# A routed two-layer network on one core: product 4 of the first layer by seven of its own blocks, and another order of the last products

## The chip, the cores and the metric

The kernel runs on one core of a Trainium2 chip. The core has a matrix engine (TensorE, PE in the profile), a vector engine (VectorE, DVE), a scalar engine (ScalarE, ACT), a general engine (GpSimd, POOL) and a sync engine (SyncE, SP) that here only issues DMAs. TensorE writes its results to PSUM, which has eight banks of 512 fp32 values in each of 128 partitions; VectorE and ScalarE read them there, GpSimd does not. Each engine runs its own queue in order and waits on semaphores that the others raise. The metric is device time in microseconds of one execution. Three runs of the kernel before gave 1569.73, 1569.85 and 1571.15 us; the median is 1569.85 us.

## The reference

The input is 4096 rows of 512 values. Each row is rotated by a quaternion product with two constant sides (in exact arithmetic one 4 x 4 mix of the row's four parts), a gate picks two of eight experts for it and two weights, and each expert takes its first 1024 rows. In an expert a row goes through two layers, and its result comes back weighted and is added to the input:

```python
logits = xf @ gate_w.T
topv, topi = jax.lax.top_k(jax.nn.softmax(logits, axis=-1), 2)
...
h = jax.nn.relu(jnp.einsum('ecd,ehd->ech', de, fc1_w) + fc1_b)   # 8 x 1024 x 2048, over 512
eo = jnp.einsum('ech,ehd->ecd', h, fc2_w) + fc2_b                # 8 x 1024 x 512, over 2048
out = x + jnp.sum(eo.reshape(E * cap, Dm)[flat_idx] * (gates * w)[:, :, None], axis=1)
```

All of it is fp32.

## The kernel before

**Order of the whole.** The routing comes first: logits, choice, ranks, and three lists of row numbers for 8 x 1024 slots. Then two generators are run in turns, `first_layers()` and `second_layers()`, which write out the engines' queues by hand (`tc.manual_schedule()`). The work is cut into 32 groups, k = 0 to 31: expert e = k // 4 and quarter g = k % 4 of its 2048 hidden units. A group's first layer (`layer1`, for group 0 `layer1_plain`) is 14 units, i = 0 to 13, one `yield` each. A group's second layer is two halves (`st0` = 0 and 2) of 7 units each. One turn is one unit of the first layer and then one unit of the second layer of the group before; in PE's queue they alternate. At turn i of group k the second layer's unit is: 0 `start` of st0 = 0 of group k-1 (with 1 and 2 still the last two of group k-2), 3 to 6 its products 1, 5, 4, 6, 7 `start` of st0 = 2, 8 product 3, 9 product 2, and 10 to 13 products 1, 5, 4, 6 of st0 = 2.

**Products of blocks.** Both layers multiply two matrices cut 2 x 2 by seven products of sums of blocks in place of eight (numbers 0 to 6; `left1`, `right2`, `sums` make the sums). A product of the first layer is 2 hidden tiles x 2 inner tiles of 128 x 128 weights against 512 slots. In the kernel before, products 0, 5 and 4 are done whole by `half` (L852): four matmuls of 512 columns. Products 1 and 6, and 3 and 2, are themselves done by seven blocks of 128 x 128 x 256 (`within`, L831, called in pairs by `pair`, L874); their sums of blocks come from `left_sub` (GpSimd, L146) and `right_sub` (VectorE, L162). The profile counts two passes for each fp32 matmul. A unit of the second layer (`product2`, L792) is four matmuls of 256 columns, eight passes.

**What VectorE does.** The first layer's results stand in SBUF in `beside` (h11, h21, r12) and `h22`. Each block's bank is added to one or two of them as soon as it is there (`add`, L886; L901, L907, L925, L917), and the next block with other signs accumulates onto the same bank: TensorE may write it again only when VectorE has read it. `chain` (L807) then makes three more sums for the second layer. The second layer's banks are added to `acc` (L1132 to L1216). The bank pools are `ps_1` (4 banks, first layer), `ps_2` (3, second layer) and `ps_x` (1, the next expert's input).

**What lies beside it.** `background` and `fetches` are lists of small steps of which `turn` (L785) runs so many after each unit as `PACE` (L1230) says for g and i, first number after the first layer's unit, second after the second layer's. In them are `chain`'s sums, the next expert's input (its rows gathered by GpSimd's indirect DMA, exchanged by 32 x 32 squares with SyncE's DMAs in `exchange`, turned by VectorE at L723 and mixed at L767, with ScalarE for the first term), and the stores of the expert before: `store` (L666) scales by the gate on ScalarE, adds to the gathered output rows on GpSimd (L669), and scatters them with an indirect DMA (L657). `TURN_OF_SUM` (L1022) says at which turns GpSimd makes the next group's four left sums.

**The end.** The last group's second layer runs alone (14 units), and the last half (`last`, L1167) is written apart: products 1, 5, 4, 6, 3, 2, where VectorE weighs each piece straight into the gathered rows (`weigh`, L650), and four scatters close the kernel. The first four tiles of the last expert still go through `store`.

Of the kernel before, what the change touches and what calls it, by code (L numbers as in the profile page):

```python
# [39 lines left out]
P = 128  # L40
D = 512
NJ = 4
E = 8
# [23 lines left out]
def kernel(  # L67
# [510 lines left out]
    vp = ctx.enter_context(tc.tile_pool(name="vp", bufs=3))  # L578
# [35 lines left out]
    beside = [hp.tile([P, 3, 2, HALF], F32, name=f"beside{i}") for i in range(2)]  # L614
    unused = [hp.tile([P, 2, HALF], F32, name=f"hidden{i}") for i in range(5)]
# [6 lines left out]
    class Rows:  # L622
# [43 lines left out]
        def store(self, st, acc):  # L666
            nc.scalar.activation(acc, acc, AF.Copy, scale=self.w[:, st : st + 1])
            r = self.rows[st]
            nc.gpsimd.tensor_tensor(r, acc, r, ALU.add)  # L669
            self.scatter(st)  # L670

    class Slots:
# [37 lines left out]
        def arrivals(self, half):  # L710

            n = PER if half == 0 else 2
            t = self.a if half == 0 else self.b
            for at in range(0, PER, n):
                for st in range(n):
                    yield lambda st=st, at=at: self.gather_ahead(t[:, st], half, at + st)
                yield from [lambda: None] * 2
                for b in range(QT):
                    yield lambda b=b, at=at: self.exchange(t, half, at, b)
                yield from [lambda: None] * 2  # L720
# [71 lines left out]
    def product2(out, st0, factors, n, first, tiles=range(2)):  # L792
# [11 lines left out]
        if st0 + 2 == PER and 1 in tiles and n in (2, 3, 4, 5):  # L804
            unused.append(factors[0][n])

    def chain(k, h22):  # L807


        h11, h21, r12 = (beside[k % 2][:, i] for i in range(3))  # L810
# [3 lines left out]
        def last():  # L814
# [7 lines left out]
            *[lambda: None] * (2 if k == NK - 1 else 0),  # L822
            last,
        ]

# [16 lines left out]
    def layer1(k, factors, subs):  # L842
# [5 lines left out]
        h11, h21, r12 = (h[:, i] for i in range(3))  # L848
# [25 lines left out]
        def pair(n, o, at, base, base_read):  # L874

            two = h[:, at : at + 2]
            t, u = bank1(f"t{n}_{k}"), bank1(f"u{n}_{k}")
            halves = t.rearrange("p (n s) -> p n s", n=2)  # L880

            def both(bank, i, first=False):
                within(bank[:, A], subs, n, i, first)
                within(bank[:, B], subs, o, i)

            def add(m, half):  # L886
                to = two[:, :, m, half]
                V.tensor_tensor(to, halves, to, ALU.add)  # L888

            within(base[:, A], subs, o, 1)  # L890
            within(base[:, B], subs, o, 2)
            base_read()
            both(t, 0, True)
            add(0, A)
            yield
            both(t, 5)
            add(0, B)
            both(u, 4, True)
            to = two[:, :, :, B]
            term = u.rearrange("p (n s) -> p n s", n=2).unsqueeze(2).to_broadcast([P, 2, 2, HS])  # L900
            V.tensor_tensor(to, term, to, ALU.add)  # L901
            yield
            both(t, 6)
            add(1, B)
            within(u[:, A], subs, n, 1, True)
            within(u[:, B], subs, n, 2)
            V.tensor_tensor(two[:, 0, 0], u, two[:, 0, 0], ALU.add)  # L907
            yield
            both(t, 3)
            add(1, A)  # L910
            relu(two[:, 0])

        def from5(m):
            nc.scalar.activation(h21[:, m], a[m], AF.Identity, bias=hi[:, m : m + 1])

        def from4(m):
            V.tensor_tensor(r12[:, m], b[m], r12[:, m], ALU.add)  # L917

        yield from pair(1, 6, 0, a[0], lambda: from5(0))
        yield  # L920
        h22 = unused.pop(0)
        b = [bank1(f"b{m}_{k}") for m in range(2)]
        for m in range(2):
            half(b[m], m, 4, True)
            V.tensor_tensor(h22[:, m], b[m], h21[:, m], ALU.add)  # L925
            if m == 1:
                from4(1)
                relu(h22)
            yield
        yield from pair(3, 2, 1, b[0], lambda: from4(0))  # L930
        chain(k, h22)
# [4 lines left out]
    def layer1_plain(k, w, x):  # L936
# [4 lines left out]
        h11, h21, r12 = (beside[k % 2][:, i] for i in range(3))  # L941
        h22 = unused.pop(0)
        for half in range(2):
# [6 lines left out]
            for at, i in ((at, i) for at in parts for i in range(NJ)):  # L950
# [22 lines left out]
                if half == 1 and done:  # L973
                    chain(k, h22)
# [3 lines left out]
    def first_layers():  # L978
# [43 lines left out]
        TURN_OF_SUM = {8: 2, 9: 0, 10: 1, 13: 3}  # L1022
        nxt = None
        for k in range(NK):
# [27 lines left out]
            if k:  # L1052
                for n, block, turns in (
                    (2, left_f[2], (2, 2, 3, 3)),
                    (3, w1_of[k][:, 1, 1], (4, 4, 5, 5)),
                ):
                    lefts[n], more = left_sub(k, n, block)
                    later(more, turns)
                if k == 1 or g == 0:
                    for n, turns in ((6, (1, 2, 2, 3)), (2, (4, 4, 5, 5)), (3, (6, 7, 8, 9))):  # L1060
                        right_subs[n], more = right_sub(xtp, e, n, xf[n])
                        later(more, turns)
# [6 lines left out]
            for i, _ in enumerate(units):  # L1069
# [3 lines left out]
                if k:  # L1073

                    if i == 8 and k + 1 < NK:
                        lefts[6], more = left_sub(k + 1, 6, left_n[6])
                        later(more, (9, 10, 11, 12))
                        lefts[1], more = left_sub(k + 1, 1, w1_of[k + 1][:, 0, 1])
                        later(more, (10, 11, 12, 13))
                        if g == NG - 1:  # L1080
                            right_subs[1], more = right_sub(xtp, e + 1, 1, xf_n[1])
                            later(more, (8, 9, 9, 12))
# [10 lines left out]
                if e + 1 < E:  # L1093

                    if (g, i) in ((0, 12 if e else 5), (1, 8)):
                        fetches.extend(nxt.arrivals(g))
                    if (g, i) in ((1, 11), (2, 9)):
# [22 lines left out]
    def second_layers():  # L1120
# [4 lines left out]

        def start(k, st0):
            e, g = divmod(k, NG)
            before = biases[e] if g == 0 else accs[st0]
            a = ps_2.tile([P, 2, DB], F32, tag="p2", name=f"a2_{k}_{st0}")
            v1 = vp.tile([P, 2, DB], F32, tag="v", name=f"v1_{k}_{st0}")  # L1130
            product2(a, st0, (hidden[k], rights[k]), 0, True)
            V.tensor_tensor(v1, a, before[:, :2, :DB], ALU.add)  # L1132
# [5 lines left out]
        for n, (k, st0) in enumerate(units):  # L1138
# [7 lines left out]
            if g == 2 and st0 == 0:  # L1146
                r = rows[e] = Rows(e)
                fetches.extend(lambda st=st, r=r: r.gather_choice(st) for st in range(SLOTS))
            if g == NG - 1 and st0 == 0:
                background.append(rows[e].weights)  # L1150
                fetches.extend(lambda st=st, r=rows[e]: r.gather_rows(st) for st in STORED)
# [10 lines left out]
            v2 = vp.tile([P, 2, DB], F32, tag="v", name=f"v2_{k}_{st0}")  # L1162
            product2(a, st0, factors, 5, False)
            V.tensor_tensor(v2, a, i12, ALU.add)
# [3 lines left out]
            if last:  # L1168
# [4 lines left out]
                for m in range(2):  # L1173
                    r.weigh(tiles[m], o11[:, m], LEFT)
                    r.weigh(tiles[m], v2[:, m], RIGHT)
                    r.weigh(tiles[2 + m], i21[:, m], LEFT)

                b = [
                    ps_2.tile([P, HALF], F32, tag="p2", name="b_top")[:, :DB],
                    ps_x.tile([P, HALF], F32, tag="xps", name="b_low")[:, :DB],  # L1180
                ]
            product2(b, st0, factors, 4, True)
            yield
            v3 = vp.tile([P, 2, DB], F32, tag="v", name=f"v3_{k}_{st0}")
            product2(a, st0, factors, 6, False)
            V.tensor_tensor(v3, a, i22, ALU.add)  # L1186
            for m in range(2) if last else [slice(0, 2)]:
                V.tensor_tensor(o22[:, m], b[m] if last else b, v3[:, m], ALU.add)
# [4 lines left out]
            if n + 1 < len(units):  # L1193
                ahead = start(*units[n + 1])
                yield
# [102 lines left out]
```

## Time and profile before

| | |
|---|---|
| median of three runs | 1569.85 us |
| the profiled execution: its time | 1569.29 us |
| the profiled execution: its span in the profile | 1567.4 us |
| granted TensorE clock, mean | 0.987 |
| PE busy | 1529.9 us, 98% of the span |
| DVE busy | 1152.7 us, 74% |
| POOL busy | 1048.7 us, 67% |
| ACT busy | 318.9 us, 20% |
| one group of steady state, k = 1 to 31 | 46.46 us |

The profile's page gives busy time by engine, then the span in 40 slices, then the groups of instructions by source line (L796 is line 796 of the kernel before). A line such as `PE b L796 <- DVE acc L1209: 0.6, 1, 0.6` in the list of waits says who waited for whom, how long in all, how often, and the longest. In the timeline a row is start, duration, engine, line, operation, output and inputs, count, and in brackets the idle time before it and who ended it. A matmul's duration in the timeline overlaps that of the next; what a stream of them costs is read from start to start.

### The profile page before, as it was taken

The numbers are of one execution on the slowest core, as the hardware profiler recorded it, in microseconds if no ns is written. First come the engines' busy times: TensorE is split into PE (matmuls) and PEld (weight loads), VectorE is DVE, ScalarE is ACT, GpSimd is POOL, SyncE is SP. The second block draws the span as 40 slices with busy tenths as digits, with TensorE's granted clock in tenths as the row PEclk, the third lists the DMA queues.
The fourth block names the chain that finished last, engine by engine and source line by source line (L and its number), as shares of the span: only waits on it lengthen the run. The fifth ranks groups of instructions, "written<-read, shape, count | busy, mean of one in ns | idle before, by whom it ended". The sixth has DMA issues, their size and how long they took to land.

```text
span 1567.4 us, 17504 instructions
## 1 busy us (share of the span) xinstructions
PE 1529.9 (98%) x6399; PEld 1190.9 (76%) x6399; DVE 1152.7 (74%) x1601; ACT 318.9 (20%) x450; POOL 1048.7 (67%) x1133
## 2 busy tenths in 40 slices
PE   5899999999999999999999999999999999999996
PEld 3677877877777787777887777787787787777785
DVE  6568886588856887578875888758886688866665
ACT  3222112221122112222112221122113121221110
POOL 1754687746977477965779468775697747794535
PEclk7899999999999999999999999999999999999998
DMA  8463123511334103531135311342133420331003
GB/s 324 160 212 94 55 68 117 140 59 55 113 97 139 62 28 114 148 116 55 33 104 159 93 55 61 121 123 79 55 102 102 139 64 28 114 107 54 11 17 106
DMA packets 79373, 152.18 MB, mean 97 GB/s; under 512 B 12022, under 2 KB 40950, under 8 KB 74168
## 3 DMA queue, kind: packets, MB, share of 16 engines
q1 hardware_dynamic: 56848, 90.24, 18.7%
q0 software_dynamic: 18048, 52.31, 10.8%
q10 hardware_dynamic: 4392, 8.52, 1.4%
q8 instruction: 50, 0.82, 0.2%
q14 instruction: 35, 0.29, 0.1%
HBM read 119.77 MB, written 25.23 MB: 93 GB/s over the span
## 4 chain that ended last, share of the span: by engine, by line
PE 91%; DVE 4%; issue 2%; DMA 2%; POOL 1%; SPq 0%; POOLq 0%; DVEq 0%
PE a L796 26%; PE b L796 20%; PE t L833 14%; PE a L854 12%; PE u L833 7%; PE b L854 7%; PE p L955 2%; PE b L833 2%; PE a L833 1%; DMA xb<-in_xt_dram 1%; DVE hidden L820 1%; DVE xa L767 1%; POOL rows L601 0%; DVE hidden L816 0%; POOL out_dram L657 0%
## 5 line engine op out<-in xcount | busy, mean ns | idle before, releaser
L796 PE MATMUL a<-t,hidden 128*128 128x256 f32 x1024 | 244.0, 382 | 5.3 <-DVE v L1186 5.2
L796 PEld LDWEIGHTS a<-t,hidden 128*128 128x128 f32 x1024 | 195.9, 191 | 58.5 <-issue 27.5
L888 DVE TENSOR_TENSOR beside<-t,beside 128x512 f32<-128x512 f32 x248 | 170.3, 687 | 94.3 <-PE t L833 90.4
L829 ACT ACTIVATE beside<-beside 128x1024 f32<-128x1024 f32 x62 | 65.5, 1057 | 558.0 <-DVE beside L888 558.0
L833 PE MATMUL t<-xsub,sub 128*128 128x256 f32 x496 | 127.9, 380 | 0.4
L796 PEld LDWEIGHTS b<-w,hidden 128*128 128x128 f32 x504 | 96.0, 190 | 38.9 <-issue 29.1
L796 PE MATMUL b<-w,beside 128*128 128x256 f32 x512 | 121.1, 380 | 0.6 <-DVE acc L1209 0.6
L796 PE MATMUL a<-t,beside 128*128 128x256 f32 x512 | 121.0, 379 | 0.0
L796 PE MATMUL a<-w,beside 128*128 128x256 f32 x512 | 121.0, 379 | 0.0
L796 PE MATMUL b<-t,hidden 128*128 128x256 f32 x504 | 119.1, 379 | 0.0
L796 PE MATMUL b<-w,hidden 128*128 128x256 f32 x504 | 119.1, 379 | 0.0
L796 PEld LDWEIGHTS b<-w,beside 128*128 128x128 f32 x512 | 97.4, 190 | 27.1 <-issue 15.7
L796 PEld LDWEIGHTS a<-w,beside 128*128 128x128 f32 x512 | 97.5, 190 | 26.2 <-issue 14.8
L854 PE MATMUL b<-x,s 128*128 128x512 f32 x248 | 116.6, 593 | 0.0
L854 PE MATMUL a<-x,s 128*128 128x512 f32 x248 | 116.6, 593 | 0.0
L854 PE MATMUL a<-xa,w 128*128 128x512 f32 x248 | 116.4, 593 | 0.0
L137 POOL TENSOR_TENSOR s<-w 128x512 f32<-128x512 f32 x31 | 39.5, 1274 | 112.7 <-PE b L854 112.7
L139 POOL TENSOR_TENSOR s<-w 128x512 f32<-128x512 f32 x31 | 39.8, 1283 | 111.3 <-PE t L833 111.3
L140 POOL TENSOR_TENSOR s<-w,s 128x512 f32<-128x512 f32 x31 | 39.4, 1270 | 107.5 <-PE t L833 101.9
L796 PEld LDWEIGHTS a<-t,beside 128*128 128x128 f32 x512 | 97.4, 190 | 13.1
L796 PEld LDWEIGHTS b<-t,hidden 128*128 128x128 f32 x504 | 96.0, 190 | 12.8
L833 PEld LDWEIGHTS t<-xsub,sub 128*128 128x128 f32 x496 | 94.0, 190 | 14.6 <-DVE beside L888 2.3
(233 smaller groups left out, 3089.4 us busy)
## 6 DMA issues: line engine op xcount, KB each, us to landing
w<-in_w_dram SPq DMA_DIRECT2D x64, 1024.0 KB, 5.1
xb<-in_xt_dram SPq DMA_DIRECT2D x8, 1024.0 KB, 9.9
out_dram<-in_x_dram ACTq DMA_DIRECT2D x1, 8192.0 KB
rows<-xa SPq DMA_DIRECT2D x112, 64.0 KB, 2.1
rows<-xb SPq DMA_DIRECT2D x224, 32.0 KB, 1.9
b<-in_b_dram POOLq DMA_DIRECT2D x8, 256.0 KB, 3.8
c<-choice,slot_cho POOLq DMA_INDIRECT x64, 2.3
rows<-out_dram,slot_tok POOLq DMA_INDIRECT x64, 3.5
```

The source lines that it names most:

```text
L137: lambda: G.tensor_tensor(s[0], w[:, 1, 0], w[:, 1, 1], ALU.add),
L139: lambda: G.tensor_tensor(s[2], w[:, 0, 0], w[:, 1, 0], ALU.subtract),
L140: lambda: G.tensor_tensor(s[3], w[:, 0, 1], s[1], ALU.subtract),
L767: V.scalar_tensor_tensor(to, t, M[:, i, j : j + 1], to, ALU.mult, ALU.add)
L796: nc.tensor.matmul(out[m] if isinstance(out, list) else out[:, m], lhsT=factors[0][n][:, c, (st0 + m) * P : (st0 + m + 1) * P], rhs=factor ...
L820: lambda: V.tensor_tensor(s2, s1, h11, ALU.subtract),
L829: nc.scalar.activation(h, h, AF.Relu)
L833: nc.tensor.matmul(out, lhsT=subs[0][n][i], rhs=subs[1][n][i], start=first, stop=True, skip_group_check=True,)
L854: nc.tensor.matmul(out, lhsT=factors[0][n][:, c, m * P : (m + 1) * P], rhs=factors[1][n][:, c, :], start=first and c == 0, stop=c == 1, sk ...
L888: V.tensor_tensor(to, halves, to, ALU.add)
L955: nc.tensor.matmul(ps[n][m][:, at], lhsT=w[:, block, i // 2, i % 2, m * P : (m + 1) * P], rhs=x.of(half, i)[:, at], start=i == 0 and at.st ...
```

## The change

Product 4 of the first layer is no longer done whole. It is done by its own seven blocks, in turns 8 to 11 (the four pieces of the diff that end in `yield`): blocks 1 and 2 go into a bank `b` (which then also takes product 2's blocks 1 and 2), blocks 0, 5, 6 and 3 go one after the other into the left half of a bank `t4`, and block 4 into the right half of the same bank. VectorE adds each from there to h22 and r12 together (`add_to_both`), and h22 now lies in `beside`. `left_sub` and `right_sub` make the sums for product 4 too. The turns of the other sums, of the gathers and exchanges for the next expert (`ARRIVE`: at turn i of g, gather or exchange of a part), of its turning and mixing, and `PACE` are set anew; `o12` and `o22` are summed in `acc` itself instead of in `v2` and `v3`.

For the last expert the output rows are gathered one group sooner, `store` is one VectorE operation (`weigh`) and a scatter, and the last half's products go in the order 1, 5, 4, 6, 2, 3 with each 256-column piece in a bank of its own.

```diff
-    beside = [hp.tile([P, 3, 2, HALF], F32, name=f"beside{i}") for i in range(2)]
-    unused = [hp.tile([P, 2, HALF], F32, name=f"hidden{i}") for i in range(5)]
+    beside = [hp.tile([P, 4, 2, HALF], F32, name=f"beside{i}") for i in range(2)]
+    unused = [hp.tile([P, 2, HALF], F32, name=f"hidden{i}") for i in range(3)]
...
         def store(self, st, acc):
+            if self.e == E - 1:
+                self.weigh(st, acc)
+                self.scatter(st)
+                return
...
+            if n == 2 and waiting:
+                background.insert(0, waiting.pop())
...
-            *[lambda: None] * (2 if k == NK - 1 else 0),
-            last,
         ]
+        (waiting if k else background).append(last)
...
+        def add_to_both(two, m, half, term):
+            to = two[:, :, m, half]
+            V.tensor_tensor(to, term.unsqueeze(1).to_broadcast([P, 2, HS]), to, ALU.add)
...
-        h22 = unused.pop(0)
-        b = [bank1(f"b{m}_{k}") for m in range(2)]
-        for m in range(2):
-            half(b[m], m, 4, True)
-            V.tensor_tensor(h22[:, m], b[m], h21[:, m], ALU.add)
-            if m == 1:
-                from4(1)
-                relu(h22)
-            yield
-        yield from pair(3, 2, 1, b[0], lambda: from4(0))
-        chain(k, h22)
+        nc.scalar.activation(h22[:, 1], h21[:, 1], AF.Copy)
+        two = h[:, 1:4:2]
+        b, t4 = bank1(f"b_{k}"), bank1(f"t4_{k}")
+        singles(b, 4, True)
+        V.tensor_tensor(h22[:, 0], b, h21[:, 0], ALU.add)
+        within(t4[:, A], subs, 4, 0, True)
+        add_to_both(two, 0, A, t4[:, A])
+        yield
+        within(t4[:, A], subs, 4, 5)
+        add_to_both(two, 0, B, t4[:, A])
+        within(t4[:, B], subs, 4, 4)
+        to = two[:, :, :, B]
+        term = t4[:, B].unsqueeze(1).unsqueeze(1).to_broadcast([P, 2, 2, HS])
+        V.tensor_tensor(to, term, to, ALU.add)
+        yield
+        three = h[:, 2:4]
+        t, u = bank1(f"t3_{k}"), bank1(f"u3_{k}")
+        singles(b, 2)
+        within(t4[:, A], subs, 4, 6)
+        add_to_both(two, 1, B, t4[:, A])
+        both(t, 3, 2, 0, True)
+        add_pair(r12, b)
+        add(three, 0, A, t)
+        yield
+        within(t4[:, A], subs, 4, 3)
+        add_to_both(two, 1, A, t4[:, A])
+        relu(h22)
+        both(t, 3, 2, 5)
+        add(three, 0, B, t)
+        both(u, 3, 2, 4, True)
+        add_twice(three, u)
+        yield
...
-        TURN_OF_SUM = {8: 2, 9: 0, 10: 1, 13: 3}
+        TURN_OF_SUM = {8: 2, 11: 0, 12: 1, 13: 3}
+        ARRIVE = (
...
+            {
+                (0, 3): [(0, 0)],
+                (0, 6): [(1, 0)],
+                (0, 13): [(0, 1)],
+                (1, 6): [(1, 1)],
+                (1, 10): [(1, 2)],
+                (1, 13): [(1, 3)],
+            },
+        )
...
-                    if (g, i) in ((0, 12 if e else 5), (1, 8)):
-                        fetches.extend(nxt.arrivals(g))
-                    if (g, i) in ((1, 11), (2, 9)):
+                    for part in ARRIVE[e > 0].get((g, i), ()):
+                        fetches.extend(nxt.arrive(*part))
+                    if (g, i) in ((1, 7), (2, 6)):
                         background.extend(nxt.steps(g - 1))
...
+            if g == (NG - 1 if e + 1 < E else 2) and st0 == 0:
+                fetches.extend(lambda st=st, r=rows[e]: r.gather_rows(st) for st in STORED)
...
+                b = banks("b_last", True)
+                product2(b, st0, factors, 4, True)
+                add(o22, b, i22)
+                product2(a, st0, factors, 6, False)
+                add(o22, a, o22)
+                for m in range(2):
+                    product2(b, st0, factors, 2, False, (m,))
+                    r.weigh(tiles[m], b[m], RIGHT)
+                    r.scatter(tiles[m])
+                for m in range(2):
+                    r.weigh(tiles[2 + m], o22[:, m], RIGHT)
+                for m in range(2):
+                    product2(a, st0, factors, 3, False, (m,))
+                    r.weigh(tiles[2 + m], a[m], LEFT)
+                    r.scatter(tiles[2 + m])
```

## The prediction, made before the changed kernel was run

> **What bounds the kernel now.** First the page's busy times and slices, then the windows by group, then the list of TensorE's waits, then the timeline for the price of one pass and of one round trip, last the ending.
>
> ```profile
> PE 1529.9 (98%) x6399; PEld 1190.9 (76%) x6399; DVE 1152.7 (74%) x1601; ACT 318.9 (20%) x450; POOL 1048.7 (67%) x1133
> ...
> PEclk7899999999999999999999999999999999999998
> ...
> 962.99:1009.45 46.46, 46.46 (x193) 36.47 (x192) 35.54 (x49) 9.64 (x14) 36.96 (x38) 1.00 0.34 108
> 1102.37:1148.83 46.46, 46.46 (x193) 36.42 (x192) 39.73 (x52) 7.08 (x10) 35.66 (x35) 1.00 0.14 46
> ...
> PE a L796 <- DVE v L1186: 5.2, 1, 5.2
> PE tok_ps L493 <- DVE A L482: 2.0, 4, 0.8
> PE b L796 <- DVE acc L1209: 0.6, 1, 0.6
> ```
>
> The two windows are one group each (columns: PE, PEld, DVE, ACT, POOL busy, clock, DMA share). PE is busy 46.46 of 46.46 us at full clock, and only two waits on VectorE fall after the routing: both in the ending, none in the 31 groups. So the groups are bound by TensorE's passes alone, and VectorE's 39.7 of 46.5 us costs nothing as long as TensorE never waits for it. A pass removed is time won; a wait added on TensorE is time lost, whole.
>
> ```profile
> 1009.46 1.88 PE L854 MATMUL a<-xa,w 128*128 128x512 f32 x4
> 1011.17 1.89 PE L796 MATMUL a<-w,beside 128*128 128x256 f32 x8
> 1012.90 1.88 PE L854 MATMUL a<-xa,w 128*128 128x512 f32 x4
> ...
> 1512.75 1.03 PE L833 MATMUL t<-xsub,sub 128*128 128x256 f32 x4
> 1513.81 0.69 DVE L888 TENSOR_TENSOR beside<-t,beside 128x512 f32<-128x512 f32 x1 [0.17 <-PE t L833]
> ...
> 490.36 0.69 DVE L1164 TENSOR_TENSOR v<-a,b 128x512 f32<-128x512 f32 x1 [0.50 <-PE a L796]
> 490.97 0.72 DVE L723 STREAM_TRANSPOSE xps<-rows 128x512 f32<-128x512 f32 x1
> 491.59 0.67 DVE L888 TENSOR_TENSOR beside<-t,beside 128x512 f32<-128x512 f32 x1
> ...
> 1523.52 0.68 DVE L1186 TENSOR_TENSOR v<-a,acc 128x512 f32<-128x512 f32 x1
> 1524.25 2.00 PE L796 MATMUL a<-t,hidden 128*128 128x256 f32 x8
> 1526.09 1.89 PE L796 MATMUL b<-w,hidden 128*128 128x256 f32 x8
> ```
>
> From start to start: four passes of 512 columns 1.71 us, 0.428 each; eight of 256 columns 1.73 us, 0.216 each. A round trip: the four passes from 1512.75 have given up their places at 1512.75 + 4 x 0.216 = 1513.61, VectorE starts at 1513.81, so 0.20 later; its 128x512 add takes 0.69; two such operations in a row start 0.61 apart, behind a transpose 0.62. VectorE ended at 1524.20 and TensorE started at 1524.25: 0.05; those eight passes then took 1.84 to the next start in place of 1.73: 0.11 to get going.
>
> **Product 4, passes.** Gone per group: 8 passes of 512 columns, 8 x 0.428 = 3.42 us. New: 7 blocks x 2 passes of 256, 14 x 0.216 = 3.02. Won: 0.40 per group, in 31 groups (k = 0 is plain) **-12.4 us**.
>
> **Product 4, the shared bank.** In turn 9 block 5 goes to t4's left half, VectorE adds it, and block 4 goes to the right half of the same bank. In the program as built block 4 carries a wait for exactly that add, though it touches other columns; no matmul stands between block 5 and it. Going through all TensorE waits on VectorE as built, the changed program has 31 such trips with nothing in between, one per group; the kernel before has one, in the ending, the 5.2 us row above. All other trips have at least a second-layer unit (1.73 us) for cover. [...] By address block 4 would run during the add and the groups would only win; by bank the trip is paid 31 times. No run here shows a collision; the built wait goes by bank, and I take that.
>
> Its price: put 0 at the end of the places of product 3 (turn 8, second layer). VectorE adds o21 from 0.20. Block 5 occupies 0 to 0.43, ready for VectorE at 0.63, but the queue is in order: its add starts at 0.20 + 0.60 = 0.80, ends 1.49, and block 4 gets going at 1.49 + 0.05 + 0.11 = 1.65 in place of 0.43: **1.22 us**. Behind block 4 stands product 2 of the second layer and all of PE's queue, with nothing to take the place. In 14 groups (g = 2 and 3, experts 0 to 6) one step of the next expert's input, a transpose or a mix, stands in VectorE's queue between o21 and the add: 0.62 to 0.66 more, **1.86**. In 8 groups (k = 1 and the g = 0) two `right_sub` steps stand ahead of o21, 0.4 to 1.5 us each in the rows of L170 to L173, partly inside the idle time ahead of it: **1.5**. The 9 others have o21 alone. Sum: 9 x 1.22 + 14 x 1.86 + 8 x 1.5 = 11.0 + 26.0 + 12.0 = **+49.0 us**. Bounds per trip: with VectorE idle, 0.20 + 0.69 + 0.05 + 0.11 = 1.05; with both subtractions slowed by GpSimd or two steps ahead, 2.6.
>
> How long the stall lasts matters once more. The row: after 5.16 us idle in the ending eight passes took 3.78 us, after 0.5 us 2.00. [...]
>
> **Product 4, the other engines.** VectorE per group: gone two adds of L925 and two of L917 (2.75 us); new one add to h22, four `add_to_both`, one add to r12 (six at 0.69) and one of 1024 at 1.23 (L901): 5.4. Net +2.6, at most 39.7 + 2.6 = 42.3 of 46: covered, provided it is spread; turns 8 to 13 hold about 16.7 us of VectorE work against 19.5 of TensorE. If that cover fails, the next late block is product 3's block 5 in turn 11 of the g = 0 groups, which needs a `right_sub` step of turn 10: 0 to 0.7 us, 8 times; I take 0, the stall of turn 9 gives VectorE that time. Four more subtractions per expert there (4 x 0.4 to 1.5) likewise. ScalarE's copy of h22's second half: 0.69 (L865), ScalarE is idle 80%. GpSimd's four sums of 128x128: 2.4 us (L155 to L158, 0.5 to 0.8) on 21 to 38 of 46 us, wanted five turns, some 17 us, later: nothing.
>
> **What is moved.** The next expert's four gathers go from turn 12 to 3 of g = 0, on GpSimd past eight row gathers and the bias load, which then come two turns later and still four turns ahead of the stores; two more go to turn 6. The exchanges (16 DMAs per half) go from turn 1 of g = 1 to turn 13 of g = 0, in SyncE's queue ahead of the next weight load, which is wanted a whole group later; turning starts in turn 7 (was 11) and 6 (was 9), six turns, 20 us, after them. The left sums 0 and 1 go to turns 11 and 12, wanted in turn 2 of the next group, 17 us later. The sum that `waiting` holds back is run after product 2 and wanted seven turns later. `v2`, `v3` gone: the same adds onto `acc`. All nothing; what they cost if late is a TensorE wait at these places.
>
> **The ending.**
>
> ```profile
> 1540.90 0.69 DVE L1216 TENSOR_TENSOR acc<-b,v 128x512 f32<-128x512 f32 x1 [1.03 <-PE b L796]
> ...
> 1547.03 2.68 DVE L652 SCALAR_TENSOR_TENSOR rows<-acc,w,rows 128x256 f32<-128x256 f32 x2
> ...
> 1552.93 3.78 PE L796 MATMUL a<-t,hidden 128*128 128x256 f32 x8 [5.16 <-DVE v L1186]
> ...
> 1561.34 0.97 POOL L657 DMA_INDIRECT out_dram<-rows,slot_add  x1 [0.30 <-issue]
> ```
>
> Product 2 of the first half ends at 1540.70; call it 0. Last pass places end at 1558.56, 17.9 later (5.2 stalled, 2.0 at half clock), the last scatter's issue at 1562.31, the span 5.1 after it. Now: VectorE does o12, four stores (0.65 each by L767), o11, two halves of o12 (0.35), six weighings (0.44 by the pairs of L652), two halves of o22: 0.2 + 0.6 + 2.6 + 0.6 + 0.7 + 2.6 + 0.7 = 8.0; four units take TensorE 6.9; so product 2 starts at 8.1 and four halves of 0.86 end at 11.6. Scatters follow 1.27 apart (rows of L657) from 9.95: the fourth starts at 13.8 and ends at 14.7, against 21.6: **-6.9 us**; from -3, if VectorE's rows stretch beside the scatters as at 1547.03, to -9. The row gathers (8 at 1.25 us on GpSimd) move into k = 31, where GpSimd is busy 21.8 of 46.46: nothing, and nothing won, since the stores waited for ScalarE's gate.
>
> **Sum.** Against the span: 1567.4 - 12.4 + 49.0 - 6.9 = 1597.1. The profiled execution is 1.9 longer than its span (1569.29), the median of the runs 0.6 longer again: 1597.1 + 1.9 + 0.6, **1599.6 us**, +1.9%.
>
> **Rivals.** (1) The trip as worked out: 1599.6, chance 0.82, its own range 1585 to 1612. (2) The kernel gets faster: one mechanism, the trip in turn 9 is short or covered. It decides at (12.4 + 6.9) / 31 = 0.62 us per group; with no trip at all 1550.6. For it: nothing else on TensorE's path is new. Against it: the wait is in the program, and the add alone is 0.69. Chance 0.05. (3) VectorE is the bound in turns 8 to 13: its queue is late by one more operation and the trips take 1.9 to 2.6, +15: 1615. For it: 86% load there, and subtractions that reach 1.5 us beside GpSimd. Against it: the stall itself gives VectorE time. Chance 0.09. (4) The clock falls in some stalls: half of 31 x 2.0, 1631. Chance 0.04.
>
> **How the numbers follow.** The time is that of (1). Below, 1.05 per trip is 32.6 in place of 49.0: 1583; above, (3). I give 1583 to 1615, which leaves out (2), (4) and the edges of (3). A measurement of this kernel tells some 0.2% from no change. Faster is (2), 0.05; the same only at 0.62 us per trip by chance, 0.01; the rest slower, 0.94.
>
> **What would show it.** In the list of waits a row of PE, line 840, for VectorE's line 901, 31 times, 40 to 55 us together, longest about 2; PE busy near 95 to 97% with the clock still full in those groups; groups of about 47.3 us (one o21) and 47.9 (with a step between); 512-column passes of the first layer 8 per group fewer; the 5 us wait of the ending gone and the last scatter some 14 to 15 us after product 2 of the first half. Wrong: the row is missing or under 0.6 us each; other rows of PE's waits on line 840 sum to more than 5 us; or the clock row falls.

## The result, and the profile after

The changed kernel takes 1648.63 us (median of four runs, 1648.17 to 1650.97) against 1569.84 us for the kernel before (four runs beside it, 1569.73 to 1571.15): ratio 1.050, 95% interval 1.049 to 1.0515. It is 79 us slower. The forecast was slower by 30 us. Its direction holds, and so does the mechanism that it put first, the trip at the shared bank; but three terms that it set at nothing were paid as well, and 1648.6 lies outside the range of 1583 to 1615.

In the changed kernel the lines lie a little lower: `product2` is L800, `within` L840, `half` L861, the adds are L891 to L904, `add_to_both` among them at L901, the first add of product 4 (blocks 1 and 2) is L933, and that of its block 4 is L942. In the lists of waits `t` stands for all banks whose names begin with t, `t4` among them. The page after, busy times and the clock row:

```profile
PE 1545.1 (94%) x6585; PEld 1231.0 (75%) x6585; DVE 1255.0 (76%) x1733; ACT 332.2 (20%) x477; POOL 1112.6 (68%) x1253
...
PEclk8889999999999999999999999999999999999999
```

The span is 1647.1 us (it was 1567.4). PE was busy 98% of it and now 94%: some 65 us of idle time (102.0 of the span for 37.5) have come onto the engine that had none in its groups before; its busy time grew by 15 us too, with fewer columns to pass. Its list of waits (who waited for whom, us in all, times, longest) says where:

```profile
PE t L840 <- DVE beside L901: 61.6, 33, 13.5
...
PE t L840 <- DVE xsub L173: 6.7, 3, 2.3
```

The first row is the trip of the forecast, TensorE's block 4 behind VectorE's add of block 5, but it holds one wait of 13.5 us. The second row was not foreseen. Five groups, one per row, from the first pass of a group to that of the next (k = 1, then g = 0, 1, 2, 3 of expert 1; columns as before: length, then PE, PEld, DVE, ACT, POOL busy, clock, DMA share, GB/s):

```profile
81.11:141.33 60.22, 45.89 (x183) 36.15 (x182) 37.07 (x57) 10.59 (x16) 25.18 (x33) 0.86 0.49 154
240.42:288.07 47.65, 46.42 (x200) 37.54 (x199) 37.46 (x56) 10.27 (x15) 42.89 (x47) 1.00 0.43 135
288.07:335.58 47.51, 46.59 (x200) 37.38 (x199) 36.75 (x41) 12.57 (x19) 38.90 (x44) 1.00 0.45 125
335.58:383.64 48.06, 46.58 (x200) 37.37 (x199) 39.49 (x52) 10.13 (x15) 22.39 (x29) 1.00 0.19 55
383.64:434.67 51.03, 48.24 (x200) 38.56 (x199) 41.77 (x54) 7.71 (x11) 37.40 (x40) 0.97 0.14 43
```

Measured in this way a group of the kernel before takes 46.56 us (k = 1: 43.11; the 46.46 given for it above is a mean over unequal groups), and a group with the new product 4 and no wait at all takes 46.15 (last but one experiment below). Against 46.15, g = 0 has lost 1.5 us, g = 1 1.4 (1.22 in most experts), g = 2 1.9, g = 3 4.9, and group 1 (against 42.7) 17.5. The clock column is under 1.00 in two of the five.

**Group 3** is where the forecast's trip is longest. Its timeline in expert 5 (start, duration, engine, line, operation, idle before):

```profile
1201.47 2.35 POOL L125 TENSOR_TENSOR x<-xc,xa 128x1024 f32<-128x1024 f32 x1
...
1202.74 1.36 DVE L170 TENSOR_TENSOR xsub<-xa 128x256 f32<-128x256 f32 x1
...
1204.02 0.68 DVE L1283 TENSOR_TENSOR acc<-a,acc 128x512 f32<-128x512 f32 x1
1204.62 0.73 DVE L771 SCALAR_TENSOR_TENSOR xb<-xps,M,xb 128x512 f32<-128x512 f32 x1
1205.28 0.67 DVE L901 TENSOR_TENSOR beside<-t,beside 128x512 f32<-128x512 f32 x1
...
1206.01 1.18 PE L840 MATMUL t<-xsub,sub 128*128 128x256 f32 x2 [2.44 <-DVE beside L901]
...
1206.99 3.14 PE L800 MATMUL b<-w,hidden 128*128 128x256 f32 x8
```

Three operations stand ahead of the L901 of 1205.28 in VectorE's queue: a subtraction for the next expert (1.36 us beside GpSimd's L125), the second layer's add o21 (L1283) and a mix. TensorE idles 2.44 us here, 2.8 in the six other experts, and afterwards its eight passes take 3.14 us in place of 1.89: the clock is at half. In each of those seven places the trace's clock record shows half clock for 3.41 us (the clock is 0.83 over the 10 us from 1206.00).

**Group 1** shows a wait of another kind. VectorE's timeline:

```profile
104.98 0.68 DVE L1200 TENSOR_TENSOR v<-a,b 128x512 f32<-128x512 f32 x1
118.96 0.73 DVE L727 STREAM_TRANSPOSE xps<-rows 128x512 f32<-128x512 f32 x1 [13.30 <-DMA rows<-xa]
...
120.36 0.69 DVE L901 TENSOR_TENSOR beside<-t,beside 128x512 f32<-128x512 f32 x1
```

SyncE's queue in the changed kernel, and what it waits for:

```profile
92.83 24.41 SPq L707 DMA_DIRECT2D rows<-xa  x16
...
SPq L707 <- DMA out_dram<-in_x_dram: 14.0, 1, 14.0
```

The same of the kernel before, and its first turning of these rows:

```profile
92.66 23.39 SPq L703 DMA_DIRECT2D rows<-xa  x16
...
SPq L703 <- DMA out_dram<-in_x_dram: 12.5, 1, 12.5
...
117.94 0.72 DVE L723 STREAM_TRANSPOSE xps<-rows 128x512 f32<-128x512 f32 x1
```

SyncE issues the 16 exchanges of expert 1's first rows until 117.24 us (116.05 before). It does not issue them in one stretch: between the sixth (ends at 96.81) and the seventh (starts at 110.86) it stands still. The seventh waits for a semaphore that the copy of the whole input into the output raises too (8 MB, issued by ScalarE's queue at 58.58). The last update that this copy makes comes at 110.84. So what is late here is SyncE's queue, not the exchange of data: an exchange behind the pause lands some 2 us after its issue (114.71 to 116.75). The kernel before has the same pause. There the turning came in turn 11, at 117.94, and had nothing to wait for; now it comes in turn 7, VectorE stands at it for 13.3 us, and every add behind it in its queue is late. The 13.5 us that the list books under L901 is this.

**Turn 13 of g = 0**, in three experts (3, 4 and 5), has the second row of the waits:

```profile
1069.66 3.22 DVE L173 TENSOR_TENSOR xsub<-x,xsub 128x256 f32<-128x256 f32 x1
...
1070.10 1.28 POOL L137 TENSOR_TENSOR s<-w 128x512 f32<-128x512 f32 x1
...
1072.94 1.22 PE L840 MATMUL t<-xsub,w 128*128 128x256 f32 x2 [2.20 <-DVE xsub L173]
```

A subtraction of 128x256, 0.42 us where no operation of GpSimd runs beside it, takes 3.22 us beside GpSimd's operations, and product 3's last blocks need it.

**The ending** went as forecast: the 5.16 us wait is gone, the longest left is 0.62 us, and the last scatter starts at 1641.05, 6.1 us ahead of the span's end (6.1 before too).

```profile
1635.28 1.99 PE L800 MATMUL b_last<-w,hidden 128*128 128x256 f32 x8 [0.62 <-issue]
1637.12 1.89 PE L800 MATMUL a<-t,beside 128*128 128x256 f32 x8
...
1641.05 0.97 POOL L657 DMA_INDIRECT out_dram<-rows,slot_add  x1 [0.31 <-issue]
```

### The profile page after: what moved, and what is told of

It reads as the page before. It is cut to its first block, busy times and chain, and to the rows that moved or that the text cites. A ratio compares the mean times of both kernels' runs of the same rounds, so it can differ in the third digit from the quotient of the medians.

```text
span 1647.1 us, 18187 instructions
## 1 busy us (share of the span) xinstructions
PE 1545.1 (94%) x6585; PEld 1231.0 (75%) x6585; DVE 1255.0 (76%) x1733; ACT 332.2 (20%) x477; POOL 1112.6 (68%) x1253
## 3 DMA queue, kind: packets, MB, share of 16 engines
q1 hardware_dynamic: 56848, 90.24, 17.5%
## 4 chain that ended last, share of the span: by engine, by line
PE 85%; DVE 9%; DMA 2%; POOL 1%; another core or an unknown queue 1%; issue 1%; SPq 1%; DVEq 0%; POOLq 0%
PE a L800 24%; PE b L800 20%; PE t L840 16%; PE a L861 13%; PE u L840 6%; PE b L840 3%; DVE beside L901 2%; PE a L840 2%; DMA xb<-in_xt_dram 1%; DVE acc L1283 1%; DVE xsub L170 1%; DVE xb L771 1%; PE p L992 1%; DVE xsub L173 1%
## 5 line engine op out<-in xcount | busy, mean ns | idle before, releaser
L836 ACT ACTIVATE beside<-beside 128x1024 f32<-128x1024 f32 x93 | 98.3, 1057 | 792.1 <-DVE beside L891 526.4
L840 PE MATMUL t<-xsub,sub 128*128 128x256 f32 x682 | 189.8, 390 | 61.6 <-DVE beside L901 61.6
L800 PE MATMUL a<-t,beside 128*128 128x256 f32 x1024 | 245.2, 383 | 0.1
L891 DVE TENSOR_TENSOR beside<-t,beside 128x512 f32<-128x512 f32 x248 | 170.6, 688 | 76.3 <-PE t L840 68.7
L800 PEld LDWEIGHTS a<-t,beside 128*128 128x128 f32 x1024 | 197.2, 193 | 41.1 <-issue 13.2
L840 PEld LDWEIGHTS t<-xsub,sub 128*128 128x128 f32 x682 | 126.1, 191 | 94.0 <-DVE beside L901 79.1
L137 POOL TENSOR_TENSOR s<-w 128x512 f32<-128x512 f32 x31 | 39.5, 1276 | 154.8 <-PE t L840 154.8
L800 PE MATMUL b<-w,hidden 128*128 128x256 f32 x504 | 130.4, 406 | 0.0
L800 PEld LDWEIGHTS b<-w,hidden 128*128 128x128 f32 x504 | 103.4, 205 | 29.1 <-issue 14.3
L800 PE MATMUL b<-w,beside 128*128 128x256 f32 x512 | 121.3, 380 | 1.4 <-DVE acc L1283 1.4
L800 PE MATMUL a<-w,beside 128*128 128x256 f32 x512 | 120.9, 379 | 0.0
L800 PE MATMUL a<-t,hidden 128*128 128x256 f32 x512 | 120.9, 379 | 0.0
L800 PE MATMUL b<-t,hidden 128*128 128x256 f32 x504 | 119.1, 379 | 0.0
L800 PEld LDWEIGHTS b<-w,beside 128*128 128x128 f32 x512 | 96.9, 190 | 29.0 <-issue 14.3
L800 PEld LDWEIGHTS a<-w,beside 128*128 128x128 f32 x512 | 97.3, 190 | 26.5 <-issue 14.8
L861 PE MATMUL a<-x,s 128*128 128x512 f32 x248 | 116.5, 592 | 0.0
L861 PE MATMUL a<-xa,w 128*128 128x512 f32 x248 | 116.4, 592 | 0.0
L800 PEld LDWEIGHTS a<-t,hidden 128*128 128x128 f32 x512 | 97.3, 190 | 13.2
L800 PEld LDWEIGHTS b<-t,hidden 128*128 128x128 f32 x504 | 95.8, 190 | 13.0
L901 DVE TENSOR_TENSOR beside<-t,beside 128x512 f32<-128x512 f32 x124 | 84.8, 684 | 22.9 <-PE t L840 19.3
L657 POOL DMA_INDIRECT out_dram<-rows,slot_add x64 | 66.9, 1045 | 37.3 <-DVE rows L652 17.5
```

The costliest lines, as they stand in the source:

```text
L137: lambda: G.tensor_tensor(s[0], w[:, 1, 0], w[:, 1, 1], ALU.add),
L657: nc.gpsimd.indirect_dma_start(out=out_of[st], out_offset=bass.IndirectOffsetOnAxis(ap=slot_add[:, s : s + 1], axis=0), in_=self.rows[st], ...
L800: nc.tensor.matmul(out[m] if isinstance(out, list) else out[:, m], lhsT=factors[0][n][:, c, (st0 + m) * P : (st0 + m + 1) * P], rhs=factor ...
L836: nc.scalar.activation(h, h, AF.Relu)
L840: nc.tensor.matmul(out, lhsT=subs[0][n][i], rhs=subs[1][n][i], start=first, stop=True, skip_group_check=True,)
L861: nc.tensor.matmul(out, lhsT=factors[0][n][:, c, m * P : (m + 1) * P], rhs=factors[1][n][:, c, :], start=first and c == 0, stop=c == 1, sk ...
```

## The experiments

Theory after these traces: nearly all of the loss is VectorE in TensorE's way at block 4, because block 4 shares block 5's bank; the length of each wait is set by what stands ahead in VectorE's queue; the longest waits, of 2.20 us and more, also cost clock (time at half clock). Rivals: the waits come from VectorE's load and would only move when block 4 is freed; or the clock falls for another reason than these waits. In the edits, `...` stands for lines left out. Times are medians, "one run" where there is only one. The kernel before, on the same chip as each set, took 1570.16 (the first four), 1569.90 (the next four) and 1571.16 us (the last).

**Block 4 ahead of the add.** TensorE no longer waits for block 5's add before block 4, and nothing else changes.

```diff
         within(t4[:, A], subs, 4, 5)
-        add_to_both(two, 0, B, t4[:, A])
         within(t4[:, B], subs, 4, 4)
+        add_to_both(two, 0, B, t4[:, A])
```

> In turn 9 product 4's block 4 is issued ahead of VectorE's add of block 5, so no block waits for a read of the other half of its bank. If the shared bank is the main loss: the 31 waits of line 840 for line 901 (53 us in the changed kernel) are gone, and with them the clock drops of the g = 3 groups (7 of about 1.85 us); what stays is the 13.5 us wait of group 1 and the g = 0 waits for a subtraction: about 1583 us, from 1578 to 1595. If VectorE's and GpSimd's greater load is the real bound and the wait only shows it: the stall moves to the next blocks, and the time stays above 1620 us.

Measured: 1584.36 us (1583.89 to 1585.20), ratio 1.009 (1.0074 to 1.0108), 64 us under the changed kernel. Its waits on VectorE outside the routing:

```profile
PE t L840 <- DVE beside L901: 12.0, 2, 11.8
PE t L840 <- DVE beside L942: 7.4, 7, 1.1
...
PE t L840 <- DVE xsub L171: 3.4, 6, 0.6
PE b L800 <- DVE acc L1283: 2.6, 6, 0.6
```

The trips are gone and did not come back elsewhere; after group 1 the clock stays full up to the end. What is left is group 1 (57.78 us, 15 over 42.7) and small waits of the full VectorE: groups of g = 0 to 3 take 46.96, 46.87, 46.36 and 47.65, some 21 us over 46.15 in all. The rows of L942 and L171 do not stand in the changed kernel's list: its stalls had covered these waits. So the 64 us are what is left after they came to light, and the trips with what followed them cost more than that.

**The turning of expert 1's rows put back** to where the kernel before has it (turns 11 and 9 with its pace, in expert 0's groups only).

```diff
-                    if (g, i) in ((1, 7), (2, 6)):
+                    if (g, i) in (((1, 7), (2, 6)) if e else ((1, 11), (2, 9))):
...
```

> Only for expert 1's input (groups 1 to 3) the turning starts at turns 11 and 9 and runs at the pace of the kernel before; all else as changed. If the 13.5 us wait of group 1 is VectorE standing at a transpose whose rows come by DMA only at about 118 us: the wait goes, with it the half clock behind it, about -17 us: 1631 us, 1627 to 1636. If the DMAs are late for all that follows and the wait only moves: 1643 us or more.

Measured: 1639.10 us (one run), 9.5 less: neither value. Group 1 falls from 60.22 to 43.93 us, but group 2 grows from 48.06 to 55.27. There TensorE waits for GpSimd:

```profile
PE a L861 <- POOL s L138: 3.3, 1, 3.3
```

GpSimd stands at a gather, which overwrites what the exchanges of the second half (`rows<-xb`) still read (its row in the waits: `xb L694 <- DMA rows<-xb`, 42.3 us in all, longest 22.9; in the changed kernel 41.5 and 23.9), with the left sums for group 2 behind it. These exchanges stand behind the late ones in SyncE's queue. So the pause holds up two engines, and freeing VectorE alone moved part of the wait to GpSimd. The rest of group 2's growth is two drops of the clock, at 135.7 and 163.0 us.

**Group 3's subtraction two turns later**, so that it no longer stands ahead of block 5's add.

```diff
                             right_subs[1], more = right_sub(xtp, e + 1, 1, xf_n[1])
-                            later(more, (8, 10, 10, 12))
+                            later(more, (10, 10, 10, 12))
```

> In the g = 3 groups the one right subtraction of turn 8 is issued in turn 10 instead. If that subtraction (slowed beside GpSimd) is what makes the g = 3 trips 2.9 us and these trips are what drops the clock: trips of about 1.7 us there, no clock drop in g = 3, 7 x (1.2 + 1.85) = -21 us: 1628 us, 1624 to 1633. If the mixing step in the queue or something else makes them long: less than -8 us, and the drops stay.

Measured: 1626.31 us (one run), 22.3 less, as expected. The trips of g = 3 idle 1.53 us in place of 2.8, the groups take 48.08 in place of 51.03, and no trip of g = 3 has a drop of the clock. Of the 2.95 us saved per group, 1.26 is shorter idle time; the rest, 1.69, is the price of one drop, about half of its 3.41 us.

**The kernel before with the changed ending alone** (last expert's stores, row gathers and order of the last products).

```diff
         def store(self, st, acc):
+            if self.e == E - 1:
+                self.weigh(st, acc)
+                self.scatter(st)
+                return
...
+                b = banks("b_last", True)
+                product2(b, st0, factors, 4, True)
+                add(o22, b, i22)
...
```

> The kernel before with the changed ending alone (last expert's rows gathered sooner, stores by VectorE, last products in the order 1, 5, 4, 6, 2, 3). If the ending brings what the prediction said: -6.9 us, 1563 us, from 1561 to 1566. If VectorE is as late there as before: within 2 us of the kernel before.

Measured: 1562.60 us (1561.57 to 1563.48), ratio 0.995 (0.9933 to 0.9967), 7.6 us less. The ending is a gain of the size that the forecast gave it.

**Block 4 in a bank of its own**, in the changed kernel's order: VectorE's add still stands ahead of it.

```diff
-        within(t4[:, B], subs, 4, 4)
+        t44 = bank1(f"t44_{k}")
+        within(t44[:, A], subs, 4, 4, True)
...
-        term = t4[:, B].unsqueeze(1).unsqueeze(1).to_broadcast([P, 2, 2, HS])
+        term = t44[:, A].unsqueeze(1).unsqueeze(1).to_broadcast([P, 2, 2, HS])
```

> The order of turn 9 stays as changed, but block 4 goes to a bank of its own in place of t4's right half (the first-layer banks then go round by nine in place of eight). If sharing the bank is the cause of the trips, and not the order of the blocks: the trips are gone as with the swap, 1584 us, 1578 to 1592. If the order alone makes TensorE wait: the 31 waits stay, over 1630 us.

Measured: 1582.46 us (one run). L901 has one wait left, group 1's:

```profile
PE t L840 <- DVE beside L901: 12.5, 1, 12.5
```

With the same operations in the same order on both engines, another bank removes all other trips. What makes TensorE wait here is the shared bank, not the order of issue nor VectorE's load; how long it waits, VectorE's load decides (the experiment on group 3's subtraction).

**The trip stretched step by step.** In g = 1 of experts 1 to 6, one to six adds of 128x256 into a scratch tile that nothing reads stand between block 5 and its add. This is work on top of the kernel's own.

```diff
+    scratch = hp.tile([P, HS], F32, name="scratch")
...
         within(t4[:, A], subs, 4, 5)
+        if g == 1 and 4 < k < 28:
+            for _ in range(k // 4):
+                V.tensor_tensor(scratch, t4[:, A], h22[:, 1, B], ALU.add)
         add_to_both(two, 0, B, t4[:, A])
```

> In the g = 1 groups of experts 1 to 6 VectorE does 1, 2, ... 6 scratch adds of 128x256 (0.34 us apart) between block 5 and its add, which lengthens TensorE's idle time there from 0.92 to about 1.26, 1.6, 1.94, 2.28, 2.62 and 2.96 us (the scratch results are used by nothing). If the clock falls by the length of the idle time: no drop up to 1.64 (as in the g = 2 groups), a drop of one 3.41 us stretch from some length between 1.64 and 2.20 on, so 3 to 4 new drops, each about 1.8 us beyond the stretch itself. [...] About 1648 + 7 + 6 = 1661 us.

Measured: 1652.77 us (one run), and the expectation missed. TensorE idled 1.25, 1.71, 2.17, 2.62, 3.08 and 3.54 us, and only the last two were followed by half clock; the waits of turn 13 in g = 0, which had all dropped the clock in the changed kernel, had none here. The fourth and the fifth trip in TensorE's timeline (these lines lie two lower), and the clock (last column but two) in a window around each:

```profile
909.24 0.70 PE L842 MATMUL t<-xsub,sub 128*128 128x256 f32 x2 [2.62 <-DVE beside L903]
909.77 1.89 PE L802 MATMUL b<-w,hidden 128*128 128x256 f32 x8
...
1107.87 0.70 PE L842 MATMUL t<-xsub,sub 128*128 128x256 f32 x2 [3.08 <-DVE beside L903]
1108.40 3.21 PE L802 MATMUL b<-w,hidden 128*128 128x256 f32 x8
```

```profile
909.00:916.00 7.00, 6.76 (x31) 5.99 (x32) 4.42 (x7) 0.00 (x0) 2.41 (x3) 1.00 0.31 85
1107.50:1114.50 7.00, 6.63 (x23) 5.52 (x24) 3.42 (x5) 0.00 (x0) 2.41 (x3) 0.76 0.28 66
```

So the length of a wait alone doesn't decide: one of 2.62 us kept the full clock here, where waits of 2.20 us at L173 in the changed kernel had half clock behind them. What decides is not shown by any run.

**All causes taken away together.** Block 4 ahead of the add, g = 3's subtraction in turn 10, and expert 1's rows gathered, exchanged and turned at the times of the kernel before.

```diff
+        within(t4[:, B], subs, 4, 4)
         add_to_both(two, 0, B, t4[:, A])
-        within(t4[:, B], subs, 4, 4)
...
-                            later(more, (8, 10, 10, 12))
+                            later(more, (10, 10, 10, 12))
...
+                    if e == 0 and (g, i) in ((0, 5), (1, 8)):
+                        for part in range(2 if g == 0 else 4):
+                            fetches.extend(nxt.arrive(g, part))
+                            fetches.extend([lambda: None] * 2)
-                    if (g, i) in ((1, 7), (2, 6)):
+                    if (g, i) in (((1, 7), (2, 6)) if e else ((1, 11), (2, 9))):
...
```

> The changed kernel with block 4 ahead of the add (as in the first experiment), expert 1's input arriving and turned at the times and pace of the kernel before, and the g = 3 subtraction of turn 8 in turn 10. If the losses found so far are all there are: the first experiment's 1584, less 12 + 3 us in group 1, less 7 x 1.3 in the g = 3 groups: 1560 us, 1555 to 1565, under the kernel before. If group 1's wait only moves to group 2 as in the second experiment: about 1568.

Measured: 1562.22 us (1561.36 to 1562.95), ratio 0.995 (0.9936 to 0.9963), as expected. Group 1 is at 42.85, group 2 at 46.62, and group 3 at 46.39; g = 0 and g = 1 are still at 46.96 and 46.86.

**The same, and product 3's subtractions in g = 0 and k = 1 begun a turn earlier.**

```diff
-                        (3, (8, 10, 10, 12)),
+                        (3, (7, 8, 10, 12)),
```

> As the run before it, and in the g = 0 groups product 3's first two right subtractions one or two turns sooner (turns 7 and 8 for 8 and 10). If the 0.57 us wait for line 171 there is only lateness of that subtraction: 7 x 0.75 = -5 us against the run before it. If VectorE is full in these turns: the wait moves to another block, within 2 us of it.

Measured: 1553.27 us (1551.87 to 1554.54), ratio 0.989 (0.9873 to 0.9903), 9.0 us less than the last; 5 were expected, since the wait that g = 1 had at L1287 (0.4 us in each of five groups) was not counted and is gone too. Groups of g = 0 take 46.15 and those of g = 1 46.18. The waits after the routing are almost gone (the one of 1.4 us lies in group 1):

```profile
PE t L840 <- DVE xsub L173: 1.4, 1, 1.4
PE b_last L800 <- DVE acc L1202: 0.6, 1, 0.6
PE b L800 <- DVE acc L1287: 0.6, 1, 0.6
```

This version is faster than both kernels. The shorter product 4 and the new ending together are worth 1.1% when next to no add of VectorE stands in front of TensorE.

**The trip alone.** The last version, with block 4 back behind the add: one line.

```diff
-        within(t4[:, B], subs, 4, 4)
         add_to_both(two, 0, B, t4[:, A])
+        within(t4[:, B], subs, 4, 4)
```

> The best version so far with one thing put back: block 4 behind VectorE's add, as in the changed kernel. If the trip has the price that it showed where nothing slow stood ahead (1.08 us with one add ahead of it, 1.65 with a step of the next expert's input more) and leaves the clock alone: 14 x 1.65 + 17 x 1.1 = 42 us on 1553: 1595 us, 1590 to 1600, and the clock full in all groups. If the clock falls at each trip: 31 x 1.8 more, over 1640 us.

Measured: 1614.87 us (1613.70 to 1616.53), ratio 1.028 (1.0266 to 1.0300), 61.6 us more than without it, and above the expected range:

```profile
PE t L840 <- DVE beside L901: 40.8, 31, 1.8
PE t L840 <- DVE xsub L173: 9.0, 4, 2.3
```

The trips by the groups' lengths come to about 48 us (1.22 in g = 1, 1.6 in g = 0, 1.7 in g = 2 and 3). The rest is what follows from the trips and was left out of the expectation: four waits at L173 in turn 13 of g = 0 (2.4 each with the restart, 9.6 us; the version without the trip has none there), and half clock in three places (about 5 us). Counted from the first pass of the group (k = 16), GpSimd's L158 and L137 start at 44.3 and 44.7 us in both versions, while VectorE's L173 starts at 42.6 without the trip, where it takes 0.65 us, and at 44.3 with it, where it takes 3.24. So the stall does not only give VectorE time, it also shifts VectorE's work against GpSimd's.

## Why the prediction was wrong

The measured loss is 50 us above the forecast. Some 41 of them are terms that the forecast set at nothing, the other 10 the length of the trips, above all in g = 3. By its own steps, from the groups' lengths against 46.15 us and from the places named above; the sum over the profiled span:

| step of the forecast | forecast, us | measured, us |
|---|---|---|
| product 4, passes | -12.4 | -12.7 |
| the shared bank, 31 trips | +49.0 | +58.8 |
| "What is moved ... All nothing": group 1 | 0 | +16.3 |
| clock, no term in the sum | 0 | +17.2 |
| turn 13 of g = 0, L173 | 0 | +7.2 |
| the ending | -6.9 | -7.2 |
| rest (routing, small waits, four longer groups of before) | 0 | +0.2 |
| sum | +29.7 | +79.8 (spans: +79.7) |

The trips, as what a group lost, are 7 x 1.5 (g = 0), 7 x 1.22 (g = 1), 7 x 1.91 and one of 1.22 (g = 2), 7 x 3.15 and one of 1.9 (g = 3) and 1.2 in group 1. Group 1 is 60.22 less 42.70 (43.11 less the 0.41 of the passes) less that 1.2.

**Right: the passes.** A group without waits is 0.41 us shorter (46.15 for 46.56), against 0.40.

**Right: that the trip is paid, and by bank.** The forecast took the wait as the program has it, by bank, against the hope that other columns of the bank would be free. The same order with another bank takes 66 us less (1582.46 for 1648.63). The runs show the wait by bank that the program contains; what would happen without it in the same bank, no run shows.

**Right: the price of a trip, for g = 0, 1 and 2.** By the groups' lengths 1.22 us in most of g = 1 (forecast 1.22), 1.5 in g = 0 (1.5), 1.9 in g = 2 (1.86).

**Mis-sized: the trip of g = 3.** The forecast put "one step of the next expert's input" ahead of the add in g = 2 and 3 alike, 1.86. In g = 3 a `right_sub` for the next expert is due in turn 8 as well; it was counted for k = 1 and g = 0 only. With 1.36 us beside GpSimd's L125 the trip costs 3.15 (the groups' excess of 4.6 to 4.9 less one drop of 1.69): 7 x 1.29 = 9 us. Two turns later for that one operation took the trips of g = 3 down to 1.9.

**Failed: "What is moved ... All nothing".** The step said that turning starts six turns, 20 us, after the exchanges. That holds while experts 1 to 6 run. Expert 1's own input, which comes while expert 0 runs, goes by another schedule: in group 1 its exchanges start at 92.8 us, and SyncE stands 14.0 us in the middle of them, at a semaphore that they share with the copy of the input. The trace of before showed it: the same pause of 12.5 us, the last of these exchanges issued by 116.05, the turning at 117.94, less than 2 us later. Only its late turn kept VectorE clear of the pause. Moving the turning four turns forward put a waiting instruction at the head of VectorE's queue: +16 us, of which the half clock after 13.5 us of idle TensorE is about 3. Putting that step back alone returns 9.5, since GpSimd waits for the exchanges of the second half, late for the same reason; with arrival and turning both put back, group 1 is at 42.85 against 42.70. That the copy's semaphore is the root is read from the times in the traces; no run gave the exchanges another one.

**Failed: the clock, which has no term in the sum.** Ten drops of 3.41 us cost some 1.7 us each, seven behind g = 3's trips and three behind L173. The forecast had two rows of the ending, 3.78 us after 5.16 us of idle time and 2.00 after 0.5, and no run of before shows that stalls between these lengths, its own of 1.2 to 1.9 us among them, cost no clock. (The row of 2.00 us that it quotes for 0.5 follows 0.12 us of idle time; the eight passes behind the wait of 0.56 took 1.97. Neither is at half clock: it is 1.00 over 1524.20 to 1530.40.) The changed kernel's trace has waits of such lengths: from group 2 on, the 23 trips of 0.78 to 1.61 us of idle time left the clock alone, and half clock followed the three waits of 2.20 to 2.27 us at L173 and the seven trips of 2.44 to 2.80. So the step failed twice: the waits were longer than forecast, and waits of 2.20 us, less than half of the row's 5.16, already cost clock.

**Failed: the late block of g = 0.** Turn 11 was named, with 0.7 us at most, and taken at 0 because "the stall of turn 9 gives VectorE that time". For turn 11 this holds: its wait, the row of L171, has 3.4 us where block 4 no longer waits, and is missing in the changed kernel. What the step left out is turn 13, with 2.4 us three times, and there the last experiment shows the opposite: the stall makes the wait.

**The rivals.** The third (VectorE is late by one more operation, trips of 1.9 to 2.6) is true in g = 3 alone, and there the trip costs 3.15. The fourth (the clock falls in half of the stalls, +31) came true in 7 of the 31; its 2.0 us per stall are the 3.78 us of the row after 5.16 us of idle time less the 1.73 of eight passes, and a drop here cost 1.7. They were weighed as alternatives; they came together, the longer trips of g = 3 bringing the drops with them, so the range was too narrow on its upper side. The loss in group 1 was in none of the rivals. One sign of being wrong that the forecast had named did show: TensorE's other waits on line 840 sum to 6.7 us, over its 5.

## What to carry to other kernels

A matmul that waited for VectorE to clear its bank cost a whole round trip in this kernel, 1.2 us with one add of 0.69 us ahead in VectorE's queue and no other matmul in between; issue the next block first, or give it another bank. Price such a trip together with everything that stands ahead in the other engine's queue at that turn, in each phase of the loop and in the first pass by its own schedule, and keep it short: in the changed kernel the trips of up to 1.61 us of idle TensorE had no drop of the clock behind them, those of 2.44 us and more had one each. Before moving a consumer forward, look in the old trace for when its transfer is really issued and lands in every phase, at what the queue that issues it waits for, and at every queue that waits for that transfer.

## What the hardware showed that was not expected

**Half clock after waits of 2.20 us.** The clock record of the changed kernel has ten short stretches at half clock, each of 3.41 us. Seven follow the trips of g = 3 (2.44 to 2.80 us of idle TensorE), and three the waits at L173 in turn 13 of g = 0 (2.20, 2.20 and 2.27 us). The 23 other trips from group 2 on, of 0.78 to 1.61 us, have none behind them. The stretched kernel does not fit an order by length: behind its trip of 2.62 us the clock is 1.00 (909.00 to 916.00 us), behind that of 3.08 us 0.76 (1107.50 to 1114.50). Why the 2.62 us cost no clock and the 2.20 us did, no run shows.

**Subtractions of VectorE from SBUF took up to eight times as long beside GpSimd's operations.** One of 128x256 with both inputs in SBUF took 0.42 us alone, 1.36 beside GpSimd's 128x1024 subtraction, and up to 3.37 (in the last experiment) beside its operations of 128x512. The add L901 at 1202.13 us, with one input in PSUM, took 0.69 beside the same L125. In both rows shown above the subtraction ends when GpSimd pauses: at 1204.10, 0.28 us after L125, and at 1072.88, 0.29 us after the last of three GpSimd operations that run without a gap (L158, L137, L673).
